# The last feed-forward layer of a chunk, traced in quarters beside the next chunk's state-space scan

## The chip, the cores and the metric

The kernel runs on one core of a Trainium2 chip. A core has five engines that run their own instruction streams: TensorE (PE in the profile, its weight loads PEld) multiplies matrices, VectorE (DVE), ScalarE (ACT) and GpSimd (POOL) work elementwise, and SyncE (SP) issues most of the DMA transfers. The metric is the device time of one execution in microseconds; lower is better.

## The reference

Two transformer-like layers on an input `x` of shape 2 x 1024 x 256, each of them attention or a state-space model followed by a feed-forward network, with a layer norm ahead of each part and a residual sum after it. Cut to what matters:

```python
# layer 0: attention, 16 heads of 128, causal, with an ALiBi bias
s = clip(q @ k.T / sqrt(128), -1024, 1024) + mask_and_bias
x = x + softmax(s) @ v @ Wo
# layer 0: feed-forward with ternary weights, 1024 hidden
h = silu(gate) * up;  x = x + rms_norm(h) @ ternary(w_proj).T
# layer 1: state space (512 channels, 16 states each)
xc = silu(conv4(in_proj(x)))
delta = softplus(dt_proj(dt_low) + bias)
h[t] = exp(delta * A) * h[t-1] + delta * B[t] * xc[t]     # for 512 x 16 products
y = (sum_n h * C[t] + xc * D) * silu(z);  x = x + out_proj(y)
# layer 1: feed-forward, of every 4 hidden values the 2 largest are kept
h = silu(x @ w_gate) * (x @ w_up);  x = x + keep_two_of_four(h) @ w_down
```

Every multiplication is done in float32.

## The kernel before

The tokens are cut into four chunks of 512 (`CH`): the two batch entries, each in two halves. Attention runs over the chunks in order, 16 heads each, four tiles of 128 queries per head (`attention`, L375). In a chunk that is the first half of its batch entry (chunks 0 and 2) a head sees up to 512 keys, in a second half (chunks 1 and 3) up to 1024. What follows attention for a chunk is `rest(k)` (L922): the ternary feed-forward, the state-space part and the kept-two feed-forward, in that order.

These are Python generators. While attention of chunk k is traced, tile by tile, `rest(k-1)` is stepped beside it (L945). Each `yield` of `rest` gives a cost, `cost` (L927) their sum, and after each tile of queries `rest` is stepped until its share of the cost has caught up with the share of tiles traced. So attention 1 has `rest(0)` beside it, attention 2 `rest(1)`, attention 3 `rest(2)`, and `rest(3)` stands alone at the end, as a tail. Attention 0 has the preparation of the ternary weights beside it.

What is traced is ordered afterwards by the framework's scheduler. It places the instructions of every engine one behind the other, mostly by the order of tracing, gives the tiles of a pool their buffers, and sets the semaphores. `tc.issue_after(i)` adds an order on one engine without a semaphore: the instructions traced in the block stand behind `i`. [...]

The state-space part (`state_space`, L505) goes as follows. The input projection (L584) yields eight blocks of 128 channels; four are convolved on VectorE (L600, L602) and pass through `Silu` (L605), four pass through `Silu` directly (L608). `steps(c)` (L531) makes delta for one of four blocks c of 128 channels by Abs, Exp and Ln. Then come 64 products (c, n), one for each block and state n. A product asks for two broadcast rows from DRAM by SP's queue (`bs`, `cs`), forms `db` = delta x · B on GpSimd (L713), `da` = exp(delta A) on ScalarE into PSUM (L727), scans on VectorE (L732), multiplies by C on GpSimd (`hc`, L746), and sums over n by transposes on TensorE into PSUM (`y`, L678). The stages list (L771) shifts these against each other; `DRAIN` is how many products later y is formed. The rings are 5 buffers for `bs`, 4 for `cs`, 4 for `db`. In the tail, `db` is made by TensorE and ScalarE instead. At the end stands the output projection `mo` (L791).

The kept-two feed-forward (`kept_two_ffn`, L860) loads the three weight matrices of 1 MB each, makes eight blocks of 128 hidden values by gate and up matmuls of 512 tokens (L432), `Silu` on ScalarE (L437) and a product on VectorE (L438); compares the four members of each group pairwise on VectorE (L899), selects (`keep_two`, L855 to L857), and projects down (`go`, L907). Of chunk 2 the projection is held back into the tail. In the ternary feed-forward, `hl` (L469) is the low part of the hidden values, made on GpSimd, as is the sum of their squares (L475).

In PSUM there are eight banks of 512 float32 columns: two for scores (`s`), three for the rest of attention (`mm`), one for `y`, and two (`r`) for all matmuls of `rest`, and for `da` too, except in the tail.

Of the kernel before, what the change touches and what calls it, by code (L numbers as in the profile page):

```python
# [17 lines left out]
P = 128  # L18
# [11 lines left out]
U = 512  # L30
# [11 lines left out]
def kernel(  # L42
# [66 lines left out]
    def layernorm_T(k, key, put, bank):  # L109
# [6 lines left out]
        def turn_two(i):  # L116
# [13 lines left out]
            put(slice(i * P, (i + 2) * P), tp)  # L130

        for i in range(UT):
# [3 lines left out]
            if (i + 1) % step == 0:  # L136
                done = slice(i + 1 - step, i + 1)
                nc.vector.tensor_scalar(rstd[:, done], mv[:, done, 1], LN_EPS, None, ALU.add)
                nc.gpsimd.tensor_tensor(rstd[:, done], rstd[:, done], minus_half[:, :step], ALU.pow)
                for j in range(done.start, done.stop, 2):  # L140
                    turn_two(j)

    def plain(pool, key):
        xT = pool.tile([P, KC, U], F32, tag="xT", name=f"xT_{key}")
        return xT, lambda t, p: nc.any.tensor_copy(xT[:, :, t], p)
# [204 lines left out]
    def scores(k, h, j, st):  # L350
# [14 lines left out]
        nm = a3.tile([P, 1], F32, tag="nm", name=f"nm_{k}_{h}_{j}")  # L365
        pace["tile"] = nc.vector.tensor_tensor_reduce(  # L366
# [75 lines left out]
    def ternary_ffn(k):  # L442
        with ExitStack() as fctx:
# [16 lines left out]
            for ic in range(NFC):  # L460
# [8 lines left out]
                nc.gpsimd.tensor_tensor(h2[1][:, ic, :], h, h2[0][:, ic, :].bitcast(F32), ALU.subtract)  # L469
# [33 lines left out]
    DRAIN = lambda k: 5 if k + 1 < len(CH) and CH[k + 1][1] == 0 else 6  # L503

    def state_space(k):  # L505
        b, u = CH[k]
        first, last, tail_end = u == 0, u == NU - 1, k == len(CH) - 1
# [3 lines left out]
        with ExitStack() as mctx:  # L511
            mc = mctx.enter_context(tc.tile_pool(name="mc", bufs=1, side="right"))
            dt_sb = mc.tile([P, DI], F32, name=f"dt_sb_{k}")
            out_sb = mc.tile([P, NDC, D], F32, name=f"out_sb_{k}")
# [14 lines left out]
            marks = []  # L529

# [38 lines left out]
            with ExitStack() as ictx:  # L569
# [6 lines left out]
                nc.sync.dma_start(out=out_sb, in_=outT.rearrange("(c p) m -> p c m", p=P))  # L576
# [34 lines left out]
                with tc.issue_after(silus[0].ins), tc.issue_after(silus[-1].ins):  # L611
                    marks.append(nc.scalar.preload_act_table_set("natural_log_exp_and_others"))
# [37 lines left out]
            more = 2 if DRAIN(k) > 5 else 0  # L650
# [6 lines left out]

            prods = [(c, n) for c in range(NDC) for n in range(DN)]
# [14 lines left out]
            ask_b, ask_c = row(brow, 0, "bs", 5), row(crow, 1, "cs", 6 if tail_end else 4)  # L673
# [15 lines left out]
            def enter(i):  # L689
# [21 lines left out]
                else:  # L711
                    db[i] = part("db", f"db_{k}_{c}_{n}", 4)
# [16 lines left out]
            def scan(i):  # L729
                c, n = prods[i]  # L730
                hs[i] = part("hs", f"hs_{k}_{c}_{n}", 6 if tail_end else 4 + more // 2)
                nc.vector.tensor_tensor_scan(  # L732
                    out=hs[i], data0=da.pop(i), data1=db.pop(i),
                    initial=0.0 if first else carry[:, n, c : c + 1],
                    op0=ALU.mult, op1=ALU.add,
                )
# [22 lines left out]
            def gate(c):  # L759
# [12 lines left out]
                (DRAIN(k), total), (-5, ask_b), (-4, prepare), (-1, enter), (0, decay), (1, scan), (2, keep), (3, weigh),  # L772
                (-1, ask_c),
            ]
            for i in range(-5, len(prods) + DRAIN(k)):
# [3 lines left out]
                if i >= 0:  # L779
                    yield 2.2  # L780
                if 0 <= i < len(prods) and i // DN + 1 < NDC:
                    c = i // DN + 1
                    if i % DN == (DN // 4 if tail_end else DN // 2):
                        parts[c] = steps(c)
                        yield 3
                    if tail_end and i % DN == DN - 5:
                        turns[c] = turned(c, parts[c][1])
            for t in range(UT):
                op = (spare(k) if t % 2 else ps_r)(f"mo_{k}_{t}")
                for c in range(NDC):  # L790
                    ended["by"] = nc.tensor.matmul(  # L791
                        op[:, :D], lhsT=xs[:, c, t * P : (t + 1) * P], rhs=out_sb[:, c, :],
# [50 lines left out]
    def keep_two(pool, key, beats, member):  # L843
# [8 lines left out]
        for j, (a, c, op_a, d, op_b, cmp, least) in enumerate(rules):  # L852
            h = member(j)
            wins = pool.tile([P, h.shape[-1]], BF16, tag="wins", name=f"wins_{key}_{j}", padded_shape=[P, 2 * U])
# [66 lines left out]

    def rest(k):  # L922
        yield from ternary_ffn(k)
        yield from state_space(k)
        yield from kept_two_ffn(k)

    def cost(k):  # L927

        own = 3 + 3 * NFC + 2 * UT + 3 + 5 * NDC + 4 + 3 * NDC + 2.2 * (DN * NDC + DRAIN(k)) + 2 * UT
        return own + 3 + 4 * NFC + 1.3 * 6 + 2.5 * 4 + 4 * UT  # L930
# [88 lines left out]
```

## Time and profile before

| what | us |
|---|---|
| median of three runs | 1869.58 (1869.01 to 1869.77) |
| the profiled execution, its own time | 1872.9 |
| its span, from the first to the last instruction | 1870.9 |
| VectorE busy | 1212.3 |
| ScalarE busy | 959.4 |
| GpSimd busy | 845.5 |
| mean granted TensorE clock | 0.981 |

The profile is of one execution. A row of a group reads: source line, engine, operation, written tile `<-` read tiles, shapes, count; then busy time in us and the mean of one in ns; then the idle time of the engine just before these instructions, and who ended it. A float32 matmul is recorded as two records. Records of TensorE overlap, so the mean of a record is longer than the time from one to the next. A row of a wait reads: who waited, for whom, us in total, times, the longest.

### The profile page before, as it was taken

The page shows a single profiled execution, that of the slowest core. Times are in us where ns is not written, and L with a number is a line of the kernel's source. Part 1 is how long each engine was busy: PE and PEld are TensorE (multiplying, and loading weights), DVE is VectorE, ACT ScalarE, POOL GpSimd, SP SyncE. Part 2 cuts the span into 40 slices and gives each one's busy share as a digit, 9 for nine tenths or more (in the row PEclk, how much of TensorE's full clock was granted, in tenths as well). Part 3 has the DMA queues.
Part 4 walks back from the last instruction along what each step waited for, and adds up shares of the span by engine and source line. Part 5 has one row for each costly group of instructions (what it writes and reads, how often), then busy time and mean ns, then how long its engine had stood idle before and what let it go on. Part 6 is the DMA issues. An engine that isn't in the chain of part 4 may idle for free. (4 is left out here: it accounts for less than half of the span.)

```text
span 1870.9 us, 24286 instructions
## 1 busy us (share of the span) xinstructions
PE 1731.3 (93%) x7984; PEld 1156.0 (62%) x7984; DVE 1212.3 (65%) x2347; ACT 959.4 (51%) x1780; POOL 845.5 (45%) x685
## 2 busy tenths in 40 slices
PE   7999999999989999997878999999999999888999
PEld 4666666455656566755556566645665655566895
DVE  5766455677786473468886465567779546446975
ACT  3445474656563562554555446465556345335742
POOL 3324031578892000429996002247889200045970
PEclk9999999999999999999999999999999999888999
DMA  6443512466662311337876324246676320112541
GB/s 188 130 141 127 195 46 86 143 201 204 208 205 83 107 51 60 119 114 231 251 245 196 121 65 133 86 132 198 204 219 203 91 93 32 70 49 73 185 128 62
DMA packets 178285, 255.99 MB, mean 137 GB/s; under 512 B 16224, under 2 KB 90976, under 8 KB 177136
## 3 DMA queue, kind: packets, MB, share of 16 engines
q1 hardware_dynamic: 177008, 241.87, 41.3%
q0 software_dynamic: 1152, 12.58, 1.8%
q8 instruction: 63, 1.03, 0.2%
q14 instruction: 62, 0.51, 0.1%
HBM read 232.04 MB, written 22.35 MB: 136 GB/s over the span
## 5 line engine op out<-in xcount | busy, mean ns | idle before, releaser
L746 POOL TENSOR_TENSOR hc<-hs,cs 128x512 f32<-128x512 f32 x256 | 363.9, 1438 | 16.1 <-PE y L678 9.3
L357 PE MATMUL s<-kT,qT 128*128 128x512 f32 (+3 forms) x768 | 304.7, 498 | 17.1 <-DVE ss L361 15.3
L370 ACT ACTIVATE ss<-ss,nm 128x128 f32<-128x128 f32 (+7 forms) x256 | 198.4, 775 | 178.0 <-DVE nm L366 168.6
L713 POOL TENSOR_TENSOR db<-du,bs 128x512 f32<-128x512 f32 x192 | 258.2, 1352 | 51.8 <-DVE hs L732 43.0
L361 DVE SCALAR_TENSOR_TENSOR ss<-s,lower 128x512 f32<-128x512 f32 (+3 forms) x384 | 204.2, 548 | 112.1 <-PE s L357 110.7
L299 PE MATMUL z<-pT,v 128*128 128x512 f32 (+3 forms) x768 | 266.1, 494 | 10.9 <-ACT pT L291 10.1
L366 DVE CUSTOM_DVE_ANT_0 ss<-ss,alibi 128x128 f32<-128x128 f32 (+7 forms) x256 | 240.6, 942 | 3.4
L727 ACT ACTIVATE da<-dl,a_neg 128x512 f32<-128x512 f32 x256 | 177.7, 697 | 118.1 <-DVE hs L732 94.3
L299 PEld LDWEIGHTS z<-pT,v 128*128 128x128 f32 x768 | 143.4, 191 | 146.2 <-issue 94.1
L291 ACT COPY pT<-pt 128x512 f32<-128x512 f32 (+3 forms) x313 | 142.9, 476 | 174.0 <-PE pt L288 172.3
L288 PE MATMUL pt<-ident,ss 128*128 128x128 f32 x1152 | 181.0, 279 | 38.6 <-DVE x L319 22.9
L288 PEld LDWEIGHTS pt<-ident,ss 128*128 128x128 f32 x1152 | 140.5, 143 | 103.1 <-DVE x L319 38.0
L732 DVE TENSOR_TENSOR_SCAN hs<-da,db 128x512 f32<-128x512 f32 x128 | 154.0, 1211 | 56.6 <-POOL db L713 27.4
L357 PEld LDWEIGHTS s<-kT,qT 128*128 128x128 f32 x768 | 129.0, 195 | 81.0 <-issue 43.9
L732 DVE TENSOR_TENSOR_SCAN hs<-da,carry,db 128x512 f32<-128x512 f32 x128 | 159.0, 1268 | 25.2 <-POOL hc L746 14.4
L319 DVE SCALAR_TENSOR_TENSOR x<-o,rr,x 128x256 f32<-128x256 f32 x256 | 108.9, 475 | 80.7 <-PE o L313 80.6
L678 PE MATMUL y<-ident,hc 128*128 128x128 f32 x1024 | 144.3, 278 | 9.6 <-POOL hc L746 9.6
L337 PEld LDWEIGHTS pv<-wv,xT_a 128*128 128x128 f32 x1024 | 126.1, 194 | 41.4 <-issue 25.4
L448 POOL DMA_DIRECT2D guT<-guT_d x4 | 2.7, 674 | 302.2 <-DVE nm L366 111.0
L337 PE MATMUL pv<-wv,xT_a 128*128 128x128 f32 x1024 | 127.3, 277 | 9.9 <-DVE carry L741 6.5
L678 PEld LDWEIGHTS y<-ident,hc 128*128 128x128 f32 x1024 | 120.7, 145 | 15.3 <-POOL hc L746 12.8
L313 PE MATMUL o<-wo,zs 128*128 128x256 f32 x512 | 123.4, 381 | 4.5 <-ACT kT L333 3.3
(199 smaller groups left out, 2617.6 us busy)
## 6 DMA issues: line engine op xcount, KB each, us to landing
cs<-bcd SPq DMA_DIRECT2D x256, 256.0 KB, 3.8
bs<-bcd SPq DMA_DIRECT2D x192, 256.0 KB, 4.4
alibi<-alibi_d SPq DMA_DIRECT2D x32, 512.0 KB, 4.5
wq<-in_wqT_dram SPq DMA_DIRECT2D x64, 128.0 KB, 3.5
wk<-in_wkT_dram SPq DMA_DIRECT2D x64, 128.0 KB, 3.2
wv<-in_wvT_dram SPq DMA_DIRECT2D x64, 128.0 KB, 2.8
wo<-in_woT_dram SPq DMA_DIRECT2D x64, 128.0 KB, 2.8
alibi<-alibi_d SPq DMA_DIRECT2D x32, 256.0 KB, 3.6
```

The costliest lines, as they stand in the source:

```text
L288: nc.tensor.transpose(tp[:, i, :], s[:, (kb0 + i) * P : (kb0 + i + 1) * P], ident)
L299: nc.tensor.matmul(zp[:, q0:], lhsT=st["v_all"][:, kb, :], rhs=st["pts"][kb // 4][:, kb % 4, q0:], start=(kb == 0), stop=(kb == last),)
L337: nc.tensor.matmul(vp[:, t, :], lhsT=xT[:, c, t * P : (t + 1) * P], rhs=st["v"][:, c, :], start=(c == 0), stop=(c == KC - 1),)
L357: nc.tensor.matmul(sp[:, :n], lhsT=st["qT"][:, j * P : (j + 1) * P], rhs=st["kT"][:, k0 : k0 + n], start=True, stop=True,)
L361: nc.vector.scalar_tensor_tensor(s[:, k0 : k0 + n], sp[:, :n], CLIP, lower[:, S - W + k0 : S - W + k0 + n], op0=ALU.min, op1=ALU.max,)
L366: pace["tile"] = nc.vector.tensor_tensor_reduce(out=s[:, :W], in0=s[:, :W], in1=st["alibi"][:, :W], scale=1.0, scalar=3.0e38, op0=ALU.add, ...
L370: nc.scalar.activation(s[:, :W], s[:, :W], AF.Exp, bias=nm, scale=-1.0, accum_out=st["rs"][:, j : j + 1])
L678: nc.tensor.matmul(yTs[c][:, t * P : (t + 1) * P], lhsT=h[:, t * P : (t + 1) * P], rhs=ident, is_transpose=True, start=start and t == 0, s ...
L713: nc.gpsimd.tensor_tensor(db[i], du, brow.pop(i), ALU.mult)
L727: nc.scalar.activation(da[i], parts[c][0], AF.Exp, scale=a_neg[:, c, n : n + 1])
L732: nc.vector.tensor_tensor_scan(out=hs[i], data0=da.pop(i), data1=db.pop(i), initial=0.0 if first else carry[:, n, c : c + 1], op0=ALU.mult ...
L746: nc.gpsimd.tensor_tensor(hc[i], hs.pop(i), crow.pop(i), ALU.mult)
```

## The change

For chunks 0 and 1 the kept-two feed-forward no longer follows the state-space part of its own chunk. A new generator, `kept_two_parts(k - 1)`, is traced beside `state_space(k)`, so the one of chunk 0 stands beside the states of chunk 1 (during attention 2), and the one of chunk 1 beside the states of chunk 2 (during attention 3). Chunks 2 and 3 keep `kept_two_ffn`. The two generators are stepped so that the same share of the costs of each is done.

`kept_two_parts` works on 256 tokens and on one half of the hidden blocks at a time, so in four quarters. It loads gate and up weights per block of 128 hidden values (two transfers of 128 KB, ring of two), twice in all, does matmuls of 256 columns, and forms silu(g) · u as (tanh(g/2) + 1) · g · u / 2 by `Tanh` on ScalarE and two instructions on VectorE. The sum with the down projection is written into `x` in place and stored from there.

To make room for it, in states with such a companion the ring of `bs` has 3 buffers, `cs` 3, `db` 3, `hs` 4 and `hc` 5, and the lag of y is 5 products. In all chunks the output projection's weights are loaded late into the buffers of `sv` and `se`. Each scan outside the tail is ordered on VectorE behind the score reduction (L366) of the tile of queries before the latest traced one. With a companion, the explicit load of the activation table for Exp and Ln is left out. In the tail's ternary feed-forward, `hl` is made on VectorE.

```diff
-    def layernorm_T(k, key, put, bank):
+    def layernorm_T(k, key, put, bank, tiles=range(UT)):
...
         nm = a3.tile([P, 1], F32, tag="nm", name=f"nm_{k}_{h}_{j}")
+        pace["front"] = pace.get("tile")
         pace["tile"] = nc.vector.tensor_tensor_reduce(
...
-                nc.gpsimd.tensor_tensor(h2[1][:, ic, :], h, h2[0][:, ic, :].bitcast(F32), ALU.subtract)
+                lower = nc.vector if k == len(CH) - 1 else nc.gpsimd
+                lower.tensor_tensor(h2[1][:, ic, :], h, h2[0][:, ic, :].bitcast(F32), ALU.subtract)
...
-    DRAIN = lambda k: 5 if k + 1 < len(CH) and CH[k + 1][1] == 0 else 6
+    DRAIN = lambda k, beside: 5 if beside or k + 1 < len(CH) and CH[k + 1][1] == 0 else 6
+    PER = 2.2
...
-                with tc.issue_after(silus[0].ins), tc.issue_after(silus[-1].ins):
-                    marks.append(nc.scalar.preload_act_table_set("natural_log_exp_and_others"))
+                if beside:
+                    marks.append(silus[-1])
+                else:
+                    with tc.issue_after(silus[0].ins), tc.issue_after(silus[-1].ins):
+                        marks.append(nc.scalar.preload_act_table_set("natural_log_exp_and_others"))
...
-            more = 2 if DRAIN(k) > 5 else 0
+            more = 2 if drain > 5 and not beside else 0
+            fewer = 1 if beside else 0
...
-            ask_b, ask_c = row(brow, 0, "bs", 5), row(crow, 1, "cs", 6 if tail_end else 4)
+            ask_b, ask_c = row(brow, 0, "bs", 5 - 2 * fewer), row(crow, 1, "cs", 6 if tail_end else 4 - fewer)
...
-                    db[i] = part("db", f"db_{k}_{c}_{n}", 4)
+                    db[i] = part("db", f"db_{k}_{c}_{n}", 4 - fewer)
...
-                nc.vector.tensor_tensor_scan(
...
+                with tc.issue_after(pace["front"].ins) if paced else nullcontext():
+                    nc.vector.tensor_tensor_scan(
...
+                if i == 3 * DN + 4:
+                    for a, tag in enumerate(("sv", "se")):
+                        o = row_of(tag, f"out{a}_{k}", 1).rearrange("p (c m) -> p c m", c=2)
+                        nc.sync.dma_start(
+                            out=o, in_=outT[a * 2 * P : (a + 1) * 2 * P, :].rearrange("(c p) m -> p c m", p=P)
+                        )
...
+    def kept_two_parts(k, pool):
...
+        order = [(tb, a, j) for tb in range(2) for a in range(2) for j in range(4)]
...
+                w[n] = pool.tile([P, 2, KC, P], F32, tag="w", name=f"gw_{k}_{n}", bufs=2)
...
+        for n, (tb, a, j) in enumerate(order):
...
+            ask(n + 1)
+            gu = ps_r(f"gu_{k}_{n}").rearrange("p (i t) -> p i t", i=2)
+            for i in range(2):
+                for c in range(KC):
+                    nc.tensor.matmul(
+                        gu[:, i, :], lhsT=w[n][:, i, c, :], rhs=xT[:, c, :],
+                        start=(c == 0), stop=(c == KC - 1),
+                    )
+            sg = pool.tile([P, W], F32, tag="sg", name=f"sg_{k}_{n}", bufs=1)
+
+            nc.scalar.activation(sg, gu[:, 0, :], AF.Tanh, scale=0.5)
+            nc.vector.scalar_tensor_tensor(sg, sg, 1.0, gu[:, 0, :], op0=ALU.add, op1=ALU.mult)
+            nc.vector.scalar_tensor_tensor(
+                hT[:, j, :], sg, 0.5, gu[:, 1, :], op0=ALU.mult, op1=ALU.mult
+            )
+            nc.scalar.activation(ab[:, j, :], hT[:, j, :], AF.Abs)
+            yield 2
...
+                for t in range(N):
+                    for i in range(4):
+                        nc.tensor.matmul(
+                            op[:, t, :], lhsT=hT[:, i, t * P : (t + 1) * P], rhs=wd_sb[:, i, :],
+                            start=(i == 0), stop=(i == 3),
+                        )
+                xt = x[k][:, tiles.start : tiles.stop, :]
+                nc.vector.tensor_tensor(xt, xt, op, ALU.add)
...
     def rest(k):
         yield from ternary_ffn(k)
-        yield from state_space(k)
-        yield from kept_two_ffn(k)
+        if 0 < k < len(CH) - 1:
+
+            with tc.tile_pool(name="gp", bufs=1, side="right") as pool:
+                both = [[state_space(k, True), states(k), 0.0], [kept_two_parts(k - 1, pool), PARTS, 0.0]]
+                while both:
+                    g = min(both, key=lambda g: g[2] / g[1])
+                    c = next(g[0], None)
+                    if c is None:
+                        both.remove(g)
+                    else:
+                        g[2] += c
+                        yield c
+        else:
+            yield from state_space(k, False)
+        if k >= len(CH) - 2:
+            yield from kept_two_ffn(k)
```

`cost` follows: the kept-two feed-forward's share is taken out of chunks 0 and 1, and `PARTS` is added to chunks 1 and 2.

## The prediction

> **What bounds the kernel now.** I read the page's first two parts, then the busy time of each engine by stage. The stages are cut where the query projections of batch half 1, 2 and 3 begin, and at 1624 us, where the last attention work ends.
>
> ```profile
> PE 1731.3 (93%) x7984; PEld 1156.0 (62%) x7984; DVE 1212.3 (65%) x2347; ACT 959.4 (51%) x1780; POOL 845.5 (45%) x685
> ```
>
> TensorE is busy for 1731 of 1871 us, so only its 140 idle us can be won unless its work shrinks. Where they lie (columns: busy us and instruction count of PE, PEld, DVE, ACT, POOL, then granted clock, DMA share, GB/s):
>
> ```profile
> 225.00:711.50 486.50, 460.93 (x2037) 293.15 (x2036) 322.20 (x613) 272.18 (x458) 223.75 (x168) 1.00 0.42 131
> 711.50:1110.50 399.00, 359.50 (x1644) 243.85 (x1643) 261.44 (x493) 201.83 (x402) 203.75 (x162) 0.97 0.51 161
> 1110.50:1624.00 513.50, 485.08 (x2119) 309.63 (x2119) 328.41 (x622) 271.49 (x465) 224.65 (x169) 0.99 0.41 129
> 1624.00:1871.00 247.00, 219.60 (x1236) 174.20 (x1234) 158.01 (x216) 111.67 (x203) 128.34 (x108) 0.93 0.33 108
> 850.00:1000.00 150.00, 121.13 (x619) 84.81 (x617) 125.41 (x180) 82.46 (x169) 148.81 (x114) 0.95 0.78 242
> 1300.00:1450.00 150.00, 139.10 (x662) 90.30 (x660) 122.36 (x215) 87.42 (x157) 133.34 (x96) 1.00 0.66 209
> ```
>
> I call the first four B (attention 1), C (attention 2), D (attention 3) and E (tail). TensorE idles 25.6, 39.5, 28.4 and 27.4 us in them. The last two rows are inside the states: in C, GpSimd is busy for 148.8 of 150 us, so there it sets the pace and TensorE idles 29 us; in D all three are close to full. TensorE's waits in C say the same:
>
> ```profile
> PE y L678 <- POOL hc L746: 9.1, 8, 3.1
> PE pt L288 <- DVE x L319: 8.0, 6, 2.4
> ```
>
> The groups that I price with:
>
> ```profile
> L746 POOL TENSOR_TENSOR hc<-hs,cs 128x512 f32<-128x512 f32 x256 | 363.9, 1438 | 16.1 <-PE y L678 9.3
> L713 POOL TENSOR_TENSOR db<-du,bs 128x512 f32<-128x512 f32 x192 | 258.2, 1352 | 51.8 <-DVE hs L732 43.0
> L732 DVE TENSOR_TENSOR_SCAN hs<-da,carry,db 128x512 f32<-128x512 f32 x128 | 159.0, 1268 | 25.2 <-POOL hc L746 14.4
> L899 DVE TENSOR_TENSOR cm<-ab 128x1024 bf16<-128x1024 f32 x18 | 21.4, 1218 | 2.6 <-ACT ab L895 2.6
> L437 ACT ACT_TABLE_LOAD x26 | 33.4, 1283 | 6.3 <-PE g_g L432 6.0
> L469 POOL TENSOR_TENSOR hl<-h,hh 128x512 fp32r<-128x512 f32 x32 | 41.1, 1285 | 73.4 <-ACT hh L468 73.3
> ```
>
> **The change, part by part.** First what TensorE needs. In the chain, four records of 512 columns take 1.72 us (0.43 each), 56 of 256 columns 12.10 (0.216), eight of 128 columns 0.89 (0.111). From these and the loop counts, a head over 1024 keys needs 21.0 us (scores 5.6, z 5.6, transposes 2.9, projections 5.2, o 1.7), one over 512 keys 12.4 (2.15, 2.15, 1.1 and the same 6.9), the 64 products of a chunk 35 (y 30.2, yb 1.8, three dt 2.6), and a kept-two feed-forward 42: 64 records x 0.43, 64 x 0.216, and the transposes. In quarters the last becomes 128 x 0.216 + 64 x 0.216: the same 42. Its weight loads double, but a load (190 ns) still fits behind a 216 ns record.
>
> *Moved work.* Feed-forward 0 leaves B (in B's window stand 30.4 us of gate and up, 4.5 of `go`, 1.4 of transposes: 36) and goes into C; number 1 leaves C and goes into D; D keeps number 2. TensorE's need: B 461 - 36 = 425. C: 359.5 less 49 (gate and up 30, the `go` of both neighbours 17.9, transposes 1.5) plus 42 = 352. D: 485 - 8 (36 `go` records of number 1 that stand there now) + 42 = 519, and 3 more because the rows count number 1 dearer than the 42: 522. E unchanged.
>
> *States spread over more attention.* The order as built shows where the first and last y transposes stand: before, from head 4 to head 11.75 in all three stages; after, heads 5 to 15.25 in B, 4.75 to 15.25 in C, 3.75 to 12.25 in D. So each stretch has 64 products beside 10.25, 10.5 and 8.5 heads instead of 7.75. Needs of the C stretch:
> - PE 10.5 x 12.4 + 35 + 36 (its part of the feed-forward) = 201, some 207 with the clock seen there.
> - POOL 64 x (1.34 + 1.34, this stage's own means) + 10 = 181.
> - DVE: attention 7.0 per head (L361 1.92, L366 2.68 + 0.32, L319 1.9, L309 0.17) = 73.5; scans 64 x 1.27 = 81; the three `steps` 11, copies and gates 7; and the feed-forward. That has 32 STT from PSUM of 256 columns at 0.41 (L361's form of that width) = 13.2; 24 comparisons, 16 x 2 `wins`, 16 selections at 256 columns, which the trace lacks. From 1218 ns at 1024 columns, between a quarter (0.305) and L857's 682 ns at 512; a line through L857's 1216 and 682 gives 0.415, which I take; `wins` 0.29 by 682 and 418: 10 + 9.2 + 6.6. With adds, copies and statistics 9.2 it is 48 against 28 before; 41 of it lies in the stretch. Sum 213.
>
> So in C the bound passes from POOL to DVE. DVE's best 50 us slice inside states was 45.4 (91%), so 213 / 0.91 = 234 us, in which PE idles 27; outside the stretch I keep 6. C = 352 + 33 = 385, 14 less than now.
>
> D stretch: PE 8.5 x 21.0 + 35 + 39 = 253; DVE 8.5 x 11.9 (L361 4.65, L366 5.2, the rest as above) + 64 x 1.21 + carries 8.8 + 45 + 15 = 247; POOL 190. 247 / 0.91 = 271: 18 idle, and 8 outside. D = 522 + 26 = 548, 34.5 more than now. B stretch: PE 250, DVE 222, POOL 190; TensorE sets the end. I keep 12 us there and 5 outside: B = 442, 44.5 less.
>
> *Silu by tanh.* 16 `Tanh` and 16 `Abs` of 256 columns, each 0.37 by L291's copy of that shape, 12 us, for 8 x 0.597 + 4 x 1.05 = 9. It also takes the table loads out of those parts. But the ternary feed-forward and the input projection now share more query tiles, and keep `Silu` beside `Exp`. The built program has 82 table loads for 66: B 22 for 28, C 26 for 12, D and E 33 for 25, one ahead. That is 16 x 1.283 = 20.5 us more ScalarE work. [...]
>
> *Clock.* C ran at 0.97 of the clock, inside its states at 0.95, where TensorE idled most. [...] If filling the gaps restores it, C gains up to 0.03 x 399 = 12 us. I take none; it serves the lower end.
>
> *Scans behind the tile before.* A scan now stands behind an L366 (0.5 to 1.5 us) on DVE. Behind it wait the exponential that wants its PSUM bank, `hc` on POOL, and five products later y on PE. Before, C's order has four scans in a row ahead of the four L319 and L361 of a head; these are the 8.0 us that transposes wait for L319. If the reduction is late, the scan is late by at most one of them, against some 3.6 us per product. I take nothing, range -8 to +8.
>
> *Rings.* `bs` from 5 to 3, `cs` and `db` to 3, the lag of y to 5. A row lands 4.4 us after its issue, and three products last 10.9 us in C: hidden, and if products come in bursts at 2.4, 7.2 against 4.4 + 1.35, still hidden. The two r banks now also hold gate/up, `go` and transposes, about 30 occupancies x 3 us beside 64 x 3: 282 of 468 bank-us, not full.
>
> *DMAs.* Per chunk 32 of 128 KB and 4 of 512 KB replace three of 1 MB: 6.3 MB for 3.1, over a stretch where the share was 0.78 and falls with the longer time. On SP's queue each weight load waits for the matmuls two parts back, and behind it stand rows; late matmuls would starve POOL, which has 50 us to spare in the C stretch. Nothing. The output weights move into `sv` and `se`, asked for 12 products ahead: nothing.
>
> *Tail.* Eight `hl` leave POOL (8 x 1.285 + 7 x 1.31, back to back) for DVE at about 0.69. ScalarE's 8 x 1.84 is next: 5 us less. E = 242. (D's last head gets 5 us of `wins` and selections among its DVE work; that is in D's 8.)
>
> **Sum** against the profiled span: -44.5 - 14 + 34.5 - 5 = -29, so 1842. Its own time is 1872.9, 2 above the span and 3.3 above the median: 1844 there, 1840 in the runs' terms.
>
> **Rivals.**
> 1. *The gaps fill* (0.15): DVE is no bound, idle in B, C, D falls to 12, 20 and 20. B 437, C 372, D 542, E 242: 1593 for 1646, 53 less, 1817; with the clock's 12 it is 1805. For: parts of B with feed-forward 0 had TensorE at 50.0 of 50 us. Against: DVE's sums above.
> 2. *VectorE becomes the bound, slower* (0.16): in C and D DVE keeps only the 83% that it had in C (125.4 of 150). Stretches 257, 298, and 267 in B: C 408, D 575, B 447, E 242, sum 1672, 26 more: 1896. It decides from 86% downward: there C is 399, D 564, B 442, E 242, sum 1647, as now. For: 83% is what both rows show; against: 91% in one slice, and before, POOL was what held it.
> 3. *The move gives back what it wins* (0.11): only the POOL-bound stretch of C improves, B keeps its idle 26 and D goes to 40: -36 -14 + 48 - 5 = -7, 1862; its lower half shades into no change.
>
> That the work isn't moved at all is excluded by the order as built.
>
> **How the numbers follow.** The main case has 0.58, own range 1822 to 1858. Below 0.2% (3.7 us, about what a measurement tells here from no change) lie some of rivals 2 and 3. Faster: 0.58 + 0.15 + 0.07 = 0.80; same 0.04; slower 0.16. Range 1806 to 1874.
>
> **What would show it.** POOL under 85% in C's states and DVE at about 90%; D longer by some 35 us and B shorter by some 45; 82 table loads; no wait of POOL on rows. Wrong if waits of PE on DVE (gate/up or transposes) grow past 60 us in C and D together.

## The result, and the profile after

The changed kernel takes 1883.69 us, median of 4 runs (1881.02 to 1885.05). The kernel before, measured beside it on the same chip, takes 1869.67 us. The ratio is 1.0062, with a 95% interval of 1.0047 to 1.0078: the change makes the kernel 0.6% slower, where I had forecast 1840 us. All ratios in this document stand against the kernel before on the same chip; where I give the difference of two changed kernels in microseconds, it is the difference of their ratios times 1870.

The first line of the page after:

```profile
PE 1735.2 (92%) x8112; PEld 1182.6 (63%) x8112; DVE 1287.9 (69%) x2521; ACT 976.6 (52%) x1828; POOL 838.6 (45%) x679
```

TensorE is busy for 1735.2 us, against 1731.3 before: its work is the same, and its idle time, 144 us for 140, is not filled. VectorE has 76 us more work, where my parts summed to some 46.

The same stages, cut at the first query projection of attention 1, 2 and 3 and at the last attention work (1639.0 us), then the two stretches from the first to the last y transpose of the states in C and in D. The columns are as before: busy us and count of PE, PEld, DVE, ACT, POOL, then granted clock, DMA share, GB/s.

```profile
224.40:658.70 434.30, 418.15 (x1908) 272.12 (x1907) 286.08 (x564) 255.09 (x441) 221.78 (x167) 1.00 0.45 139
658.70:1060.50 401.80, 354.97 (x1682) 250.37 (x1681) 306.46 (x583) 214.91 (x425) 208.57 (x163) 0.97 0.53 168
1060.50:1639.00 578.50, 539.03 (x2331) 354.02 (x2331) 386.75 (x744) 292.51 (x508) 224.41 (x173) 0.97 0.41 131
1639.00:1879.30 240.30, 216.85 (x1241) 170.73 (x1239) 166.38 (x227) 111.56 (x203) 118.63 (x98) 0.96 0.30 97
798.00:1057.60 259.60, 217.94 (x1080) 158.90 (x1079) 227.85 (x374) 129.26 (x276) 178.49 (x134) 0.95 0.66 204
1225.00:1512.00 287.00, 259.17 (x1221) 175.69 (x1219) 220.38 (x402) 149.36 (x274) 179.54 (x128) 0.98 0.54 169
```

| stage | before | forecast | after | PE idle: forecast | after | PE busy: forecast | after |
|---|---|---|---|---|---|---|---|
| B | 486.5 | 442 | 434.3 | 17 | 16.2 | 425 | 418.2 |
| C | 399.0 | 385 | 401.8 | 33 | 46.8 | 352 | 355.0 |
| D | 513.5 | 548 | 578.5 | 26 | 39.5 | 522 | 539.0 |
| E | 247.0 | 242 | 240.3 | | | | |

(Before is cut as in the prediction. Cut at the first and last records themselves, B was 486.4 us, C 398.8, D 512.6 and E 247.9; the experiments are held against these.) B and E did what was forecast, and some more. C should have lost 14 us and gained 3; D should have gained 34.5 and gained 65. Of the 38 us that the four stages lie above the forecast, 26 are idle time of TensorE (C 14, D 13.5, B less 1), 13 are TensorE work that I had set too low, and E takes 2 back.

In the C stretch GpSimd is now at 69% (178.5 of 259.6) where it had been at 99%, and VectorE at 88%. The bound did pass from one to the other, as forecast, but the stretch lasts 260 us and not 234. In the D stretch VectorE is at only 77% (220.4 of 287) and TensorE, at 90%, is the busiest. TensorE's longest waits in C (us in total, times, longest) are as small as before:

```profile
PE pt L289 <- DVE x L320: 9.5, 4, 4.2
PE y L688 <- POOL hc L758: 9.0, 2, 5.4
```

GpSimd in its turn waits for VectorE, over the whole span:

```profile
POOL db L723 <- DVE hs L744: 147.5, 52, 9.0
POOL hc L758 <- PE y L688: 49.7, 16, 10.9
```

The first was 43.0 us before, the second 9.3; of the 147.5, 56.9 lie in B, 37.1 in C and 53.4 in D. The weights that the quarters load twice are in time: TensorE waits for none of them in C or D. The costliest groups that answer to those of the forecast, shapes kept apart where the line has several:

```profile
L758 POOL TENSOR_TENSOR hc<-hs,cs 128x512 f32<-128x512 f32 x256 | 351.5, 1387 | 66.7 <-PE y L688 49.7
L744 DVE TENSOR_TENSOR_SCAN hs<-da,carry,db 128x512 f32<-128x512 f32 x128 | 160.1, 1270 | 11.9 <-ACT da L737 4.0 <-PE db L711 3.1 <-POOL hc L758 2.7
L992 DVE TENSOR_TENSOR cm<-ab 128x256 bf16<-128x256 f32 x48 | 35.8, 772 | 0.5 <-ACT ab L989 0.5
L875 DVE TENSOR_TENSOR wins<-cm 128x256 bf16<-128x256 bf16 x32 | 21.6, 676 | 0.4
L876 DVE TENSOR_TENSOR wins<-wins,cm 128x256 bf16<-128x256 bf16 x32 | 17.3, 540 | 0.4
L877 DVE SCALAR_TENSOR_TENSOR gh<-wins,gh 128x256 f32<-128x256 bf16 x32 | 20.5, 641 | 0.5
L986 DVE SCALAR_TENSOR_TENSOR gh<-sg,gu 128x256 f32<-128x256 f32 x32 | 13.1, 410 | 0.2
L372 ACT ACT_TABLE_LOAD x32 | 41.1, 1283 | 2.0 <-DVE nm L368 1.5
```

Here is the term that stands out. I had priced a comparison of 256 columns (L992) at 0.415 us, a sum for `wins` (L875, L876) at 0.29 and a selection (L877) at 0.415. They took 0.772, 0.676 and 0.540, and 0.641. The four groups make 95.2 us in the two chunks, for 51.6 in my sum. The form right beside them that reads PSUM (L986) took 0.410, which is what I had given it.

### The profile page after: what moved, and what is told of

The parts are those of the page before. It is cut to its first block, busy times and chain, and to the rows that moved or that the text cites. A ratio compares the mean times of both kernels' runs of the same rounds, so it can differ in the third digit from the quotient of the medians.

```text
span 1879.3 us, 24876 instructions
## 1 busy us (share of the span) xinstructions
PE 1735.2 (92%) x8112; PEld 1182.6 (63%) x8112; DVE 1287.9 (69%) x2521; ACT 976.6 (52%) x1828; POOL 838.6 (45%) x679
## 5 line engine op out<-in xcount | busy, mean ns | idle before, releaser
L758 POOL TENSOR_TENSOR hc<-hs,cs 128x512 f32<-128x512 f32 x256 | 351.5, 1387 | 66.7 <-PE y L688 49.7
L723 POOL TENSOR_TENSOR db<-du,bs 128x512 f32<-128x512 f32 x192 | 266.4, 1390 | 177.5 <-DVE hs L744 147.5
L300 PE MATMUL z<-pT,v 128*128 128x512 f32 (+3 forms) x768 | 271.7, 502 | 16.0 <-ACT pT L292 12.2
L368 DVE CUSTOM_DVE_ANT_0 ss<-ss,alibi 128x128 f32<-128x128 f32 (+7 forms) x256 | 244.5, 957 | 3.0
L744 DVE TENSOR_TENSOR_SCAN hs<-da,db 128x512 f32<-128x512 f32 x128 | 153.9, 1209 | 28.3 <-ACT da L737 22.7
L320 DVE SCALAR_TENSOR_TENSOR x<-o,rr,x 128x256 f32<-128x256 f32 x256 | 109.0, 476 | 90.5 <-PE o L314 90.5
L688 PE MATMUL y<-ident,hc 128*128 128x128 f32 x1024 | 151.0, 279 | 14.9 <-POOL hc L758 14.9
L331 PE MATMUL pq<-xT_a,wq 128*128 128x512 f32 x256 | 122.7, 601 | 0.7 <-ACT xT_a L146 0.7
```

What stands on the lines that cost most here:

```text
L300: nc.tensor.matmul(zp[:, q0:], lhsT=st["v_all"][:, kb, :], rhs=st["pts"][kb // 4][:, kb % 4, q0:], start=(kb == 0), stop=(kb == last),)
L368: pace["tile"] = nc.vector.tensor_tensor_reduce(out=s[:, :W], in0=s[:, :W], in1=st["alibi"][:, :W], scale=1.0, scalar=3.0e38, op0=ALU.add, ...
L688: nc.tensor.matmul(yTs[c][:, t * P : (t + 1) * P], lhsT=h[:, t * P : (t + 1) * P], rhs=ident, is_transpose=True, start=start and t == 0, s ...
L723: nc.gpsimd.tensor_tensor(db[i], du, brow.pop(i), ALU.mult)
L744: nc.vector.tensor_tensor_scan(out=hs[i], data0=da.pop(i), data1=db.pop(i), initial=0.0 if first else carry[:, n, c : c + 1], op0=ALU.mult ...
L758: nc.gpsimd.tensor_tensor(hc[i], hs.pop(i), crow.pop(i), ALU.mult)
```

## The experiments

My theory after this result: C and D are late because VectorE has some 44 us more to do there than I thought, since its small instructions run beside GpSimd's products. The rivals: the smaller rings starve the products; the new order of the scans makes them late; the table loads delay the exponentials; D alone is the fault, since its attention is the long one.

### The disputed durations by themselves

A kernel of its own, which computes nothing of the reference: the forms in question, sixteen of each, once alone and once beside GpSimd products issued back to back.

```
nc.vector.tensor_tensor(ge_q, a[:, :256], b[:, :256], ALU.is_ge)               # L92
nc.vector.tensor_tensor(w_q, h[:, :256], g[:, :256], ALU.add)                  # L98
nc.vector.scalar_tensor_tensor(p_q, b[:, :256], 1.0, pt[:, :256], ...)         # L106, pt in PSUM
nc.vector.tensor_tensor_scan(out=sc, data0=pt, data1=b[:, :512], ...)          # L108, pt in PSUM
nc.gpsimd.tensor_tensor(busy[1 + i % 3], a[:, :512], sc, ALU.mult)             # L118, 130 of them
```

> Computes none of the reference: VectorE's forms by themselves, 16 each, once with GpSimd idle and once beside GpSimd products of 512 columns. Theory 'shared access': an instruction of VectorE that reads two operands from SBUF waits for GpSimd's products. Then the 256-column comparison takes some 0.40 us alone and 0.75 to 0.80 beside GpSimd, the 256-column addition of bf16 0.29 and 0.55 to 0.70, the 1024-column comparison 1.22 and more than 1.4; the form with one PSUM operand stays at 0.41 in both, and the scan at 1.21. Theory 'narrow is dear': the 256-column forms take 0.65 to 0.77 in both halves.

The groups of this kernel; `_alone` and `_both` in the names tell the two halves apart:

```profile
L92 DVE TENSOR_TENSOR geq_alone<-xs 128x256 bf16<-128x256 f32 x16 | 6.8, 423 | 0.0
L92 DVE TENSOR_TENSOR geq_both<-xs,start 128x256 bf16<-128x256 f32 x16 | 23.6, 1477 | 0.0
L96 DVE TENSOR_TENSOR gef_alone<-xs 128x1024 bf16<-128x1024 f32 x16 | 19.8, 1234 | 0.0
L96 DVE TENSOR_TENSOR gef_both<-xs,start 128x1024 bf16<-128x1024 f32 x16 | 36.4, 2277 | 0.0
L106 DVE SCALAR_TENSOR_TENSOR pq_alone<-xs,pt 128x256 f32<-128x256 f32 x16 | 7.3, 454 | 0.0
L106 DVE SCALAR_TENSOR_TENSOR pq_both<-start,pt 128x256 f32<-128x256 f32 x16 | 6.5, 408 | 0.0
L108 DVE TENSOR_TENSOR_SCAN sc_alone<-pt,xs 128x512 f32<-128x512 f32 x16 | 19.6, 1226 | 0.5
L108 DVE TENSOR_TENSOR_SCAN sc_both<-pt,start 128x512 f32<-128x512 f32 x16 | 19.6, 1223 | 0.5
L113 POOL TENSOR_TENSOR busy<-xs,sc_alone 128x512 f32<-128x512 f32 x1 | 1.3, 1261 | 101.6 <-DVE sc_alone L108 101.6
L118 POOL TENSOR_TENSOR busy<-xs,sc_alone 128x512 f32<-128x512 f32 x130 | 212.2, 1668 | 0.0
```

Alone, a comparison of 256 columns takes 423 ns: my price of 415 was right for an idle neighbour. Beside a busy GpSimd it takes 1477. I had expected 750 to 800, which is what the changed kernel shows, but there GpSimd is not busy all the time (69% of the C stretch). The surcharge of a comparison is 1054 ns at 256 columns and 1043 at 1024: it belongs to the instruction, not to its width, so that by these rows one instruction split into four pays it four times. (Of the seven two-operand forms tried, six pay 1032 to 1056 ns; the selection of 1024 columns pays 732.) The instructions with one operand in PSUM pay nothing (L106, 454 ns alone and 408 beside, and the scan L108, 1226 and 1223). The products lose as well, from 1261 ns, of which there is one record, to 1668 in the mean. The other theory, that narrow instructions are dear by themselves, falls. The rows show that both engines lose time and that the place of one operand decides; what the two share no run shows. I had weighed no such surcharge in the prediction.

The trace of the kernel before shows it too, in a line that I had used as an average. The same reduction over ALiBi (both operands in SBUF) and the same clip (one in PSUM), in C, first ahead of the states and then inside them, by form:

```profile
L366 DVE CUSTOM_DVE_ANT_0 ss<-ss,alibi 128x128 f32<-128x128 f32 x4 | 1.1, 279 | 0.0
L361 DVE SCALAR_TENSOR_TENSOR ss<-s,lower 128x128 f32<-128x128 f32 x4 | 1.1, 286 | 3.1 <-PE s L357 3.1
```

```profile
L366 DVE CUSTOM_DVE_ANT_0 ss<-ss,alibi 128x128 f32<-128x128 f32 x6 | 6.7, 1115 | 0.0
L361 DVE SCALAR_TENSOR_TENSOR ss<-s,lower 128x128 f32<-128x128 f32 x6 | 1.7, 277 | 0.0
```

The first pair is from 720 to 830 us, the second from 850 to 1000. The reduction of 128 columns goes from 279 to 1115 ns, the clip stays. The comparisons of the kernel before stood in the parts without products (all eighteen took 1211 to 1226 ns), and so their row of 1218 ns at 1024 columns was a price without a neighbour.

### Selection left out

```diff
-            for i in range(j):
-                nc.vector.tensor_tensor(
-                    cm[:, PAIRS.index((i, j)), :], ab[:, i, :], ab[:, j, :], ALU.is_ge
-                )
...
-                for c in keep_two(
...
+                for c in range(4):
```

> The changed kernel without the comparisons and the selection of the quarters (their output keeps all four values). That takes some 95 us from VectorE by the trace after, 47 from each of two chunks. Theory 'VectorE is overfilled by the quarters': attention 2 and attention 3 shorten by 15 to 25 us each, the time is 1835 to 1855. Theory 'something else sets the end' (order of scans, rings, loads of tables): less than 12 us in all, 1872 or more.

1842.17 us, ratio 0.9831 (0.9816 to 0.9846): 43 us below the changed kernel for 95.2 us of VectorE work, 0.45 us for each. B hardly moves (436.1 for 434.3). C and D of this kernel, by stage:

```profile
659.90:1042.50 382.60, 352.61 (x1683) 250.66 (x1682) 262.41 (x516) 213.44 (x420) 202.81 (x163) 0.97 0.58 176
1042.50:1601.00 558.50, 532.49 (x2331) 350.58 (x2330) 349.59 (x675) 291.04 (x504) 222.58 (x173) 0.98 0.44 136
```

C falls by 19 us and D by 20, and TensorE's idle time in them from 46.8 and 39.5 to 30.0 and 26.0, about the 33 and 26 that I had forecast with 52 us of that work still in. Though VectorE is at 67% of D as a whole, what it has to do there counts. This run leaves out the work and the step between gate and projection together; the next two keep the step.

### The operand in PSUM

The comparisons keep their number, width and place, and read the gate's product from PSUM in place of the absolute values.

```diff
-                    cm[:, PAIRS.index((i, j)), :], ab[:, i, :], ab[:, j, :], ALU.is_ge
+                    cm[:, PAIRS.index((i, j)), :], ab[:, i, :], gu[:, 0, :], ALU.is_ge
```

> The changed kernel, with the second operand of the 48 comparisons in the quarters taken from the gate's product in PSUM and not from the absolute values in SBUF (its output is not the reference's: it compares with another value). Count, width and place of the instructions stay. Theory: a VectorE instruction waits behind a running GpSimd instruction when both its operands are in SBUF, and not when one is in PSUM: 0.40 to 0.45 us each for the 0.77 of the changed kernel, 16 to 18 us less VectorE work, and by the rate of the run without selection (42 us for 95) 7 to 8 us less: 1876. Rival: 0.77 is what a comparison of this width takes beside so much other work, whatever its operands: 0.7 to 0.8 again and 1884.

The group of the comparisons in this kernel:

```profile
L992 DVE TENSOR_TENSOR cm<-ab,gu 128x256 bf16<-128x256 f32 x48 | 18.3, 412 | 0.0
```

412 ns for 772: the surcharge is gone with one operand's place, and 17.5 us of the comparisons' time with it (VectorE as a whole is busy for 12.1 us less). The time is 1871.70 us, ratio 0.9989 (0.9972 to 1.0006), 14 us below the changed kernel, where 7 to 8 was expected. Its twelve runs spread from 1863.78 to 1877.16, though, and in the profiled execution, one of the longer ones, C is 3.7 and D 4.3 us shorter, which is what was expected. A comparison here no longer waits for the absolute values of its own part, but that wait was 0.5 us in all. So the surcharge on these instructions is real in the kernel, and it costs time; how much lies between 8 and 14 us.

### Fewer and wider instructions

The selection of a quarter in 12 instructions in place of 18, with the same columns in all.

```diff
-            for i in range(j):
-                nc.vector.tensor_tensor(
-                    cm[:, PAIRS.index((i, j)), :], ab[:, i, :], ab[:, j, :], ALU.is_ge
-                )
+            if j:
+                for i in ([0, 1, 2] if j == 3 else []):
+                    nc.vector.tensor_tensor(
+                        cm[:, PAIRS.index((i, i + 1)) : PAIRS.index((i, i + 1)) + 3 - i, :],
+                        ab[:, i : i + 1, :].to_broadcast([P, 3 - i, W]), ab[:, i + 1 : 4, :], ALU.is_ge,
+                    )
...
+                        nc.vector.tensor_tensor(wn, cm[:, 0:5:4, :], cm[:, 1:6:4, :], ALU.add)
```

> The changed kernel with the same comparisons and selection in fewer, wider instructions of VectorE: three comparisons of 768, 512 and 256 columns for six of 256, five sums and differences for eight; so 12 for 18 per quarter, 48 fewer in all. If the cost is the wait behind GpSimd, paid per instruction, 48 x 0.35 to 0.5 us = 17 to 24 us leave VectorE, and at the rate that the run without selection showed (42 us for 95) the time falls by 7 to 12 us, to some 1872 to 1877. If the cost goes with the columns, it stays within 3 us.

1874.25 us, ratio 1.0003 (0.9993 to 1.0013), 11 us below the changed kernel. Its comparisons:

```profile
L993 DVE TENSOR_TENSOR cm<-ab 128x768 bf16<-128x768 f32 x8 | 9.3, 1158 | 0.0
L993 DVE TENSOR_TENSOR cm<-ab 128x512 bf16<-128x512 f32 x8 | 7.6, 946 | 0.0
L993 DVE TENSOR_TENSOR cm<-ab 128x256 bf16<-128x256 f32 x8 | 6.5, 813 | 0.0
```

Three instructions of 768, 512 and 256 columns take 2.92 us; six of 256 took 4.63. The whole selection takes 77.7 us for 95.2. The kernel comes back to the time before the change, and the selection is still done.

### One chunk moved

Only the feed-forward of chunk 0 goes beside the states of chunk 1; that of chunk 1 stays where it was.

```diff
-        if 0 < k < len(CH) - 1:
+        if k == 1:
...
-        if k >= len(CH) - 2:
+        if k >= 1:
```

> The changed kernel with only the feed-forward of chunk 0 moved, beside the states of chunk 1; chunk 1's follows its own states as before, and chunk 2 has the old rings. If the move costs about alike in both places: attention 1 stays at 434 us, attention 2 takes 401.8 plus 42 to 50, attention 3 some 515, the time is 1865 to 1880. If the move into attention 2 (where GpSimd was the bound) is the good half: below 1862. If the move into attention 3 is the good half: above 1890.

1877.61 us, ratio 1.0019 (1.0012 to 1.0027). B loses 50.3 us and C, which keeps its own feed-forward, gains 61.9, more than I had expected (to 460.7, for 444 to 452); D stays at 512.6 and the tail loses 7. So the first move costs 11.6 us in B and C, of which the tail's edit pays 7 back, and the second another 8 by the ratios: the rival that lays it all on D's long attention falls. (The order of the scans is in this run too.)

### The order of the scans

Taken out of the changed kernel, and put alone into the kernel before:

```diff
-            paced = not tail_end
+            paced = False
```

> The changed kernel without the order that puts scans behind tiles of queries. Theory 'scans come too late': GpSimd waits less for scans (147 us in all with the order) and the time falls by 8 us or more below 1884. Theory 'VectorE is overfilled': the order only says who waits, and the time stays within 5 us of 1884, or rises because transposes wait for VectorE's sums again.

```diff
+        pace["front"] = pace.get("tile")
         pace["tile"] = nc.vector.tensor_tensor_reduce(
...
-                nc.vector.tensor_tensor_scan(
+                with tc.issue_after(pace["front"].ins) if not tail_end else nullcontext():
+                    nc.vector.tensor_tensor_scan(
```

> The kernel before with one part of the change: each scan outside the tail ordered behind the score reduction of a tile of queries. Without the order the changed kernel was 2.1% slower than before and 30 us slower than with it. If the order is good by itself (VectorE serves the tiles of queries first), 5 to 20 us less than before. If it only pays where VectorE is overfilled, within 4 us; if it starves GpSimd, which is the bound in attention 2 here, 5 us or more slower.

Without it the changed kernel takes 1914.33 us, ratio 1.0209 (1.0192 to 1.0226), 27 us more. In its trace B is 31.7 us longer (466.0 for 434.3), where GpSimd now waits 60.5 us for y in place of 4.1; C is 3.0 longer and D 3.5 shorter. Alone in the kernel before it gives 1866.63 us, ratio 0.9969 (0.9957 to 0.9981), 6 us less. D of that kernel, to be held against the 512.6 us of the kernel before:

```profile
1106.90:1613.60 506.70, 479.12 (x2115) 306.82 (x2114) 323.28 (x615) 273.10 (x470) 224.37 (x169) 1.00 0.41 130
```

The order of the scans is a gain, most of all in B of the changed kernel. That it is what made C and D late is refuted: without it they come out within 4 us.

### The smaller rings

Alone in the kernel before, for chunks 1 and 2:

```diff
-    DRAIN = lambda k: 5 if k + 1 < len(CH) and CH[k + 1][1] == 0 else 6
+    DRAIN = lambda k: 5 if 0 < k < len(CH) - 1 or k + 1 < len(CH) and CH[k + 1][1] == 0 else 6
...
-            ask_b, ask_c = row(brow, 0, "bs", 5), row(crow, 1, "cs", 6 if tail_end else 4)
+            few = 1 if 0 < k < len(CH) - 1 else 0
+            ask_b, ask_c = row(brow, 0, "bs", 5 - 2 * few), row(crow, 1, "cs", 6 if tail_end else 4 - few)
...
-                    db[i] = part("db", f"db_{k}_{c}_{n}", 4)
+                    db[i] = part("db", f"db_{k}_{c}_{n}", 4 - few)
```

> The kernel before with one part of the change: the smaller rings for rows and products and the shorter lag, in chunks 1 and 2. If the rings are no limit, within 4 us of before. If GpSimd as the bound of attention 2 lives from the deeper rings, 8 us or more slower, with waits of GpSimd for rows or scans grown by as much.

1890.52 us, ratio 1.0096 (1.0081 to 1.0111): 18 us more, where I had said nothing; 10.7 of them lie in D and 3.6 in C. Waits over the whole span of this kernel, and then those of the kernel before:

```profile
DVE hs L733 <- POOL db L714: 60.6, 47, 3.7
POOL hc L747 <- PE y L679: 23.5, 10, 7.2
POOL db L714 <- DMA bs<-bcd: 21.0, 19, 3.1
```

```profile
DVE hs L732 <- POOL db L713: 29.3, 25, 3.5
POOL hc L746 <- PE y L678: 9.3, 6, 2.8
POOL db L713 <- DMA bs<-bcd: 8.2, 5, 2.7
```

Each scan waits for its product and each product for its row: there the products come just in time, and a shorter ring is felt. Whether it is felt in the changed kernel had to be asked there. Leaving out the selection makes space for five rows of B:

```diff
-            ask_b, ask_c = row(brow, 0, "bs", 5 - 2 * fewer), row(crow, 1, "cs", 6 if tail_end else 4 - fewer)
+            ask_b, ask_c = row(brow, 0, "bs", 5), row(crow, 1, "cs", 6 if tail_end else 4 - fewer)
...
-                (drain, total), (-5 + 2 * fewer, ask_b), ...
+                (drain, total), (-5, ask_b), ...
```

> The changed kernel without the comparisons and the selection of the quarters (its output is not the reference's: chunks 0 and 1 keep all four values), and with the space that this leaves given to the rows of B: five buffers asked for five products ahead, as before the change, where the changed kernel has three. Theory: the smaller rings cost in the changed kernel what they cost in the kernel before (18 us for rows of B, of C, products and the lag together), and the rows of B are the larger half of it: 8 to 15 us under the 1842 us of the run without selection, the waits of products on rows gone, stretches C and D shorter. Rival: in the changed kernel VectorE sets the pace, rows are there in time, and three buffers are enough: 1842, within 2 us.

1841.42 us, ratio 0.9844 (0.9828 to 0.9861), against 1842.17 (0.9831) with three rows: no difference. The waits do shrink, those of scans for products from 12.8 to 6.8 us and those of products for rows from 11.3 to 5.6, but nothing that sets the time hangs on them. In the changed kernel itself scans wait 4.4 us for products in all, since VectorE is late. The rings are a cost in the kernel before; for the rows of B there is none to be seen in the changed one. The rings of `cs` and `db` and the lag of y were not tried in the changed kernel.

### Silu in the quarters

```diff
-            nc.scalar.activation(sg, gu[:, 0, :], AF.Tanh, scale=0.5)
-            nc.vector.scalar_tensor_tensor(sg, sg, 1.0, gu[:, 0, :], op0=ALU.add, op1=ALU.mult)
...
+            nc.scalar.activation(sg, gu[:, 0, :], AF.Silu)
+            nc.vector.tensor_tensor(hT[:, j, :], sg, gu[:, 1, :], ALU.mult)
```

> The changed kernel with Silu in the quarters in place of Tanh. It takes 16 of 32 VectorE instructions per chunk of 0.41 us away (13 us in both chunks, by the rate of the run without selection 6 us), and brings table loads beside the Exp of the queries: up to two for each of the 32 parts, 64 x 1.28 = 82 us of ScalarE work in C and D. Theory: ScalarE has room on average (53% busy) but the exponentials wait behind the loads: 5 to 25 us slower than the changed kernel. Rival: ScalarE hides the loads, VectorE's relief counts: 3 to 6 us faster, 1878.

1881.91 us, ratio 1.0054 (1.0039 to 1.0070): the same as the changed kernel within the intervals. The trace has 137 table loads for 82 (27 for 1 stand ahead of the quarters' own activation, L984), and ScalarE is busy for 1036.6 us, 60 more. VectorE's relief did not come: its count is 2517 for 2521 although 32 instructions were taken out, and ScalarE's only 27 higher with 55 loads more, so that some 28 instructions, by the counts, changed from ScalarE to VectorE. VectorE is busy 5.7 us less. Neither side was right: 55 more loads and that little relief come out even, and which share each has stays open. That the 16 added loads of the changed kernel are its trouble finds no support here.

### The tail's lower halves, and both winning parts together

```diff
-                nc.gpsimd.tensor_tensor(h2[1][:, ic, :], h, h2[0][:, ic, :].bitcast(F32), ALU.subtract)
+                low = nc.vector if k == len(CH) - 1 else nc.gpsimd
+                low.tensor_tensor(h2[1][:, ic, :], h, h2[0][:, ic, :].bitcast(F32), ALU.subtract)
```

> The kernel before with one part of the change: the low part of the tail's hidden values made on VectorE. If the tail's ternary stage was set by GpSimd's fifteen instructions in a row, 4 to 7 us less (ratio 0.9965 to 0.998). If ScalarE's three passes or the load of the weights set it, within 1 us.

In the kernel before this gives 1868.02 us, ratio 0.9975 (0.9966 to 0.9983): 4.5 us less, 5 forecast. With the order of the scans beside it, and nothing else of the change:

> The kernel before with only the two parts of the change that won when each was alone: scans ordered behind tiles of queries (6 us) and the tail's eight lower halves on VectorE (4.5 us). Theory: they lie in different stages (B to D, and E), so they add: 0.9945 of the kernel before, some 10 us less, E 4 to 5 us shorter and D some 8 shorter. Rival: part of the pacing's gain is a tail that starts in better order, so that they overlap: 6 us less, 0.997.

1860.13 us, ratio 0.9936 (0.9921 to 0.9951), 12 us below the kernel before and the fastest of those that leave nothing out. D and E of it, by stage:

```profile
1105.10:1610.90 505.80, 477.60 (x2115) 306.16 (x2114) 324.11 (x614) 273.50 (x470) 223.40 (x169) 1.00 0.40 131
1610.90:1854.90 244.00, 217.96 (x1241) 171.61 (x1239) 166.24 (x227) 111.89 (x203) 119.88 (x100) 0.94 0.33 109
```

They add up as parts in different stages should: in the profile D is 6.8 us shorter than before, B 3.8, E 3.9, C 1.9.

## Why the prediction was wrong, step by step

**The price of the selection: the step that failed.** "From 1218 ns at 1024 columns ... a line through L857's 1216 and 682 gives 0.415, which I take; `wins` 0.29": these are durations beside an idle GpSimd, used for a place beside its products. The durations in place were 0.54 to 0.77, and "10 + 9.2 + 6.6" for a chunk was 47.6 (half of 95.2) for 25.8. My bounds for the unknown cost (a quarter of the wide row to the half-width row, 0.305 to 0.682) did not hold the comparison's 0.772 either, because both ends came from the same kind of place.

The same fault stood in the sum a second time. The score reduction has both operands in SBUF too, and my 2.68 us for a head's four, 0.67 each, was an average over C with and without products. In the C stretch:

```profile
L368 DVE CUSTOM_DVE_ANT_0 ss<-ss,alibi 128x384 f32<-128x384 f32 (+3 forms) x44 | 42.2, 960 | 0.3
```

At 0.96 for 0.67 these 44 make 13 us more. With some 22 for the selection, my sum of 213 becomes 248; the durations of all VectorE instructions in the stretch add up to 249.

**The divisor 0.91.** Neighbouring instructions of VectorE overlap in the trace, so that durations add up to more than busy time: 249 us of durations in the C stretch are 228 us busy. My 0.91 was a share of busy time (45.4 us of a slice of 50, whose durations add up to 50.9), and I divided a sum of durations by it. In C the stretch took 260 us, 0.96 by durations and 0.88 by busy time; a correct sum divided by 0.91 would have said 274. So the two faults had opposite signs there, and that the forecast of C was not further off is luck.

**What the misprice cost.** 44 us of selection by the 0.45 of the run without it is 20 us; by the run with fewer instructions (11 us for 17.5) it is 28; by the run with the PSUM operand 20 from its C and D (8 us for 17.5) or 35 from its medians (14). These are estimates from those runs; the miss in the stages is 38. So it is half of the miss or more, and by itself brings the main case from 29 us won to somewhere between 9 won and 6 lost.

**TensorE's need of a feed-forward.** "The same 42" came from single records of the chain. The two in quarters take 61.6 us of gate and up and 29.5 of `go` in the trace, with transposes some 47 each. Since 3 us of this were already allowed for in D, it makes 7 of the 13 us by which TensorE's work was set too low; the other 6 stay open. That quarters cost TensorE no more than whole ones was right: 61.6 and 29.5 for two, against 60.5 and 29.9 for half of the four before.

**D.** Here the sum came out and the rate did not. The durations of VectorE in the D stretch add up to 245 us for my 247, by luck: the stretch held three of the four quarters (18 of the 24 comparisons), at dearer prices. TensorE has 259 as forecast at 253. Still the stretch is 287 us and not 271, 0.85 by durations for my 0.91, and PE idles 28 for 18. So VectorE is not D's bound on average; yet 20 us go when the selection goes, and 4.3 when only its operand moves. Which short stretches decide it I have not shown. Nor was my reckoning that the two banks `r` are not full tried by any run: in D scans wait 22.7 us for `da`, which shares these banks with the quarters, for 12.3 before (over the whole span 26.7 for 25.5). That rival stands.

**The order of the scans.** "I take nothing, range -8 to +8": 6 us won in the kernel before, within the range. It is worth 27 in the changed kernel, which the range didn't foresee; the loss without it lies in B, where GpSimd waits for y.

**Rings.** "Hidden" was wrong for the kernel on which I reckoned it: 18 us. I had held a landing of 4.4 us against three products, bursts too, and looked at C alone, where 3.6 of the 18 lie. The waits show rows and products late all the same; which of the sizes does it, and why that reckoning doesn't cover it, I have not shown. For the rows of B the "hidden" was right in the changed kernel without its selection.

**What was right.** B, in its direction and nearly in its size: 52 us where 44.5 was forecast; 7 of the difference are TensorE work that I had counted too high. The tail, 6.7 us for 5, and 4.5 in the run of that edit alone, though each of the eight took 995 ns on VectorE for my 0.69. The passing of the bound from GpSimd to VectorE in C. The table loads, 82 as counted, at 1283 ns each with 2.0 us of idle time before the 32 of the row above; the upper part of my range allowed for dearer ones, which no run shows. In C outside the stretch TensorE idles 5.2 us (46.8 less 41.7) for the 6 that I kept, and 55 more loads, with Silu in the quarters, cost no time on balance (ratio 1.0054 for 1.0062). The clock stayed at 0.97 in C and gave nothing; whether filled gaps would restore it was not shown, since TensorE idled 46.8 us there for 39.5 before. That GpSimd would not wait for rows is nearly so: 10.4 us over the whole span for 8.2.

**The rivals.** That VectorE becomes the bound, the second, came true in C, where it was busy for 88% and C took 401.8 us for the 399 of its point of decision; but its reason, a VectorE that is not kept busy, was not the one: it was kept busy with dearer work. In D its reason fits better, 0.85 by durations where it decides from 0.86 downward, and D took 578.5 for its 564, 17 us of TensorE work that I had not counted among them; but that VectorE bounds D no row shows. The sign I had named as wrong, waits of PE on DVE of over 60 us in C and D, did not come: the lateness shows in GpSimd's waits for VectorE instead, 90.5 us in C and D.

## What to carry to other kernels

Take the duration of an instruction from the stretch in which it will run, and look at the shapes apart by what the neighbour engine does at that time: here a comparison of 256 columns took 423 ns beside an idle GpSimd and 772 among its products. The VectorE instructions with both operands in SBUF that were tried paid 0.7 to 1.06 us beside back-to-back products of GpSimd, a narrow comparison as much as a wide one (1.054 at 256 columns, 1.043 at 1024), so small ones are better merged, given an operand in PSUM, or left in parts without products. Hold sums of durations against durations: here they exceed VectorE's busy time by some 10% (249 us for 228 in the C stretch, 245 for 220 in D's). And when a large change loses, try its small parts alone: two of them were worth 12 us.

## What I had not expected of the hardware

- A comparison of two SBUF operands on VectorE, alone and beside GpSimd's products: 423 and 1477 ns for 256 columns, 1234 and 2277 for 1024. A `scalar_tensor_tensor` of 256 columns with one operand in PSUM: 454 and 408. The scan with PSUM input: 1226 and 1223.
- The GpSimd product itself: 1261 ns alone (one record), 1668 in the mean beside such instructions.
- In the kernel, a comparison of 256 columns went from 772 to 412 ns by the place of one operand.
